# Even quarters for a one-hot table, two block products interleaved, and two more multiplications of zeros in a two-layer graph attention kernel

## The chip, the core and the metric

The kernel runs on one core of one Trainium2 chip. Times are microseconds of device time for one execution. The names of the engines in the profile are PE (TensorE, matrix products), PEld (its weight loads), DVE (VectorE), ACT (ScalarE), POOL (GpSimd) and SP (SyncE, which issues most transfers).

## The reference

A graph of 512 nodes has 16,896 edges (`src`, `dst`), sorted by `dst`, one self loop for each node among them. Two graph attention layers run over it; the second has one head, and the result is added to `x` and normalised.

```python
def gat_layer(x, W, a_s, a_d, b, edge_index, concat):
    h = (x @ W).reshape(n, H, C)
    alpha_s = jnp.einsum('nhc,hc->nh', h, a_s)
    alpha_d = jnp.einsum('nhc,hc->nh', h, a_d)
    e = leaky_relu(alpha_s[src] + alpha_d[dst], 0.2)
    e = jnp.exp(e - segment_max(e, dst)[dst])
    alpha = e / (segment_sum(e, dst)[dst] + 1e-16)
    return segment_sum(h[src] * alpha[:, :, None], dst) + b
...
h = elu(gat_layer(x, W1, ...))       # x 512x768, W1 768x6144, 8 heads of 768
out = gat_layer(h, W2, ...)          # W2 6144x768, 1 head
return layernorm(x + out)
```

## The kernel before

The kernel never walks the edges one by one. It first counts, for each pair of destination and source, how many edges there are (`cnt`, 512x512), and then treats attention as dense matrices, head by head: projection of `x`, logits, a softmax weighted with the counts, the aggregation, and the second layer's product of this head, all summed up. Large products are done by a scheme with seven block products instead of eight, P1 to P7, each on blocks of 256 rows by 384 by 384; a block product has two halves of 128 rows (`i` = 0 and 1) and three chunks of 128 along the sum (`HK` = 3). A product in float32 of one chunk shows in the trace as two passes of TensorE, so one half of a block product is six passes.

Instructions are not reordered: each engine runs its own in the order in which the Python code issues them, and waits for others by semaphores where data require it. The changed stage is the first 62 us, in which three things are interleaved by hand on all engines:

- **Loading and turning x.** x arrives in pieces, in the order written out at the start of the kernel: left halves of row blocks 0 and 1, the left half of the first weights (three chunks), right halves of the row blocks, and so on. `turn_x(t, r)` transposes a half row block by three products with the identity (line 213) into a bank of the pool `mm`, and ScalarE copies it into `xT` (line 214). Before that, `keep_warm(n)` issues n multiplications of zeros of 128x128 by 128x512 (line 184) that nobody reads.
- **The first projection** (`first_projection`, head 0). Its list `items` holds fourteen steps, P1, P2, P5, P3, P6, P7 and P4, each for `i` = 0 and 1; a step multiplies (line 309, through `product`) and empties its bank, on ScalarE by a copy (line 430) or on VectorE by an addition (line 432). P1 has banks of the pool `held`, since P6, P7 and P4 add to them later. `turns` says after which step more of x is turned: two groups after the first step, four after the third.
- **Counting.** Edges lie in 132 chunks of 128 (`EC`). For each chunk there is a one-hot of its sources (`os`, 128x512, made on VectorE at line 528 or on ScalarE at line 526, from a pool of 32 buffers) and one or two one-hots of its destinations within blocks of 32 nodes, in the table `od`. TensorE multiplies the two (line 554) and sums over chunks. VectorE makes `od` in four quarters (`destinations`, line 507) by comparing `rel`, the destination less the block's first node, with `offsets`. A quarter has 33 chunks; the columns written are rounded outwards to even ones, so each quarter's write has 34 columns, one of which belongs to a neighbour:

```python
def destinations(lo, hi):
    lo, hi = lo // 2 * 2, (hi + 1) // 2 * 2
```

The loop over nine `batches` issues, in turn: the quarter of `od` that is new, the VectorE one-hots of the batch, some additions for later products (`extra`, among them `inside`, lines 513 and 514, which checks the destinations, and the sums of x, lines 289 to 292), the steps of the projection up to `wants[n]` with ScalarE's one-hots between them, and the counting (`count`). On ScalarE the step `nidx` (line 611), which its one-hots need, stands after the first step of the projection.

Of the kernel before, what the change touches and what calls it, by code (L numbers as in the profile page):

```python
# [8 lines left out]
F32 = mybir.dt.float32  # L9
F16 = mybir.dt.float16  # L10
BF16 = mybir.dt.bfloat16
# [3 lines left out]
ALU = mybir.AluOpType  # L15
# [21 lines left out]
def gat_pass(  # L37
# [16 lines left out]
    nc = tc.nc  # L54
    P = 128
    N, D = x.shape
    H = a_src1.shape[0]
    E = src.shape[0]
    NT = N // P
    DC = D // P  # L60
    HALF = D // 2
    EC = E // P
    EH = EC // 2
    HK = DC // 2
# [14 lines left out]
    ohp = counting.enter_context(tc.tile_pool(name="onehot", bufs=1))  # L79
# [3 lines left out]
    held = counting.enter_context(tc.tile_pool(name="held", bufs=2, space=bass.MemoryType.PSUM))  # L83
# [88 lines left out]
    B0, additions0 = sums_by_dma(W1[0], w1_0, "w1")  # L172
# [9 lines left out]
    def keep_warm(n):  # L182
        for _ in range(n):
            nc.tensor.matmul(idle, zeros[:, :P], zeros, start=True, stop=True)

    keep_warm(5)
    nodes = ohp.tile([P, N], F16, name="nodes")
    nc.gpsimd.iota(nodes, pattern=[[1, N]], base=0, channel_multiplier=0,
                   allow_small_or_imprecise_dtypes=True)
# [8 lines left out]
    for j in range(2):  # L198
        nc.vector.tensor_reduce(picks[:, j:j + 1], ident.rearrange("p (j k) -> p k j", k=32)[:, j, :], axis=AX.X,
                                op=ALU.add)  # L200
# [8 lines left out]
    def turn_x(t, r):  # L209

        ps = mm.tile([P, 512], F32, name="mm")
        for k in range(HK):
            nc.tensor.transpose(ps[:, k * P:(k + 1) * P], x_sb[:, t, (r * HK + k) * P:(r * HK + k + 1) * P], ident)  # L213
        nc.scalar.copy(xT[:, r * HK:(r + 1) * HK, t * P:(t + 1) * P],
                       ps[:, :HALF].rearrange("p (k n) -> p k n", n=P))


    general = flag is None
    idx_f = ohp.tile([EH, 2, 2, P], F32, name="idx_f")
    if general:  # L220
        nc.vector.tensor_copy(idx_f, idx_i)
        idx = ohp.tile([P, 2, EC], F32, name="idx")
        psi = tr.tile([P, 512], F32, name="tr")
        for j in range(2):
            for r in range(2):
                nc.tensor.transpose(psi[:, (2 * j + r) * EH:(2 * j + r + 1) * EH], idx_f[:, j, r, :],
                                    ident[:EH, :EH])
        nc.vector.tensor_copy(idx, psi[:, :2 * EC].rearrange("p (j c) -> p j c", j=2))
    else:

        B = 32
        blocks = []
        for c in range(EC):
            m = (c + 0.5) * P * N / E
            b = int(m // B)
            slack = 2 + 16 * (m / N * (1 - m / N)) ** 0.5
            lo, hi = b - (m - b * B < slack), b + ((b + 1) * B - m < slack)
            blocks.append(range(max(lo, 0), min(hi, N // B - 1) + 1))  # L240
        assert max(map(len, blocks)) <= 2


        base = ohp.tile([P, 2, EC], F32, name="base")
        for k in range(2):
            firsts = [b[k] if k < len(b) else None for b in blocks]
            lo = 0
            while lo < EC:
                hi = lo + 1
                while hi < EC and firsts[hi] == firsts[lo]:  # L250
                    hi += 1
                nc.gpsimd.memset(base[:, k, lo:hi], float(2 * N if firsts[lo] is None else firsts[lo] * B))
                lo = hi
        offsets = ohp.tile([P, B, 2, EC // NT + 1], F16, name="offsets")
        nc.vector.tensor_copy(offsets.rearrange("p b k c -> p b (k c)"),
                              nodes[:, :B].unsqueeze(2).to_broadcast([P, B, 2 * (EC // NT + 1)]))
        nc.vector.tensor_copy(idx_f, idx_i)
        turn_x(0, 0)
        turn_x(1, 0)
        psi = tr.tile([P, 512], F32, name="tr")  # L260
        for j in range(2):
            for r in range(2):
                nc.tensor.transpose(psi[:, j * EC + r * EH:j * EC + (r + 1) * EH], idx_f[:, j, r, :], ident[:EH, :EH])
        rel = ohp.tile([P, 2, EC], F16, name="rel")
        nc.vector.tensor_tensor(rel, psi[:, :EC].unsqueeze(1).to_broadcast([P, 2, EC]), base, op=ALU.subtract)
        idx = ohp.tile([P, EC], F32, name="idx")
        nc.vector.tensor_copy(idx, psi[:, EC:2 * EC])

# [140 lines left out]
        nc.vector.tensor_tensor(cnt[:, t, :], steps[:, 1:], steps[:, :N], op=ALU.subtract)  # L409
        nc.scalar.activation(absent[:, t, :], cnt[:, t, :], AF.Relu, bias=far, scale=NO_EDGE)  # L410

    def first_projection(h, XA, B_):


        HS[h] = hs = hpool.tile([P, NT, D], F32, name="hs")
        new_alpha(h)
        bank = {}

        def step(p, over, i, out, op):
            def multiply():  # L420
                if over is None:
                    bank[p, i] = (held if p == "P1" else mm).tile([P, 512], F32, name="held" if p == "P1" else "mm")
                else:
                    bank[p, i] = bank[over, i]
                product(bank[p, i], XA, B_, p, i, over is None)

            def empty():
                ps, o = bank[p, i][:, :HALF], out(i)
                if op is None:
                    nc.scalar.copy(o, ps)  # L430
                else:
                    nc.vector.tensor_tensor(o, o, ps, op=op)
            return multiply, empty, op is not None

        steps = [
            ("P1", None, lambda i: hs[:, i, L], None),
            ("P2", None, lambda i: hs[:, i, L], ALU.add),
            ("P5", None, lambda i: hs[:, 2 + i, R], None),
            ("P3", "P5", lambda i: hs[:, i, R], None),
            ("P6", "P1", lambda i: hs[:, i, R], ALU.subtract),  # L440
            ("P7", "P1", lambda i: hs[:, 2 + i, R], ALU.subtract),
            ("P4", "P1", lambda i: hs[:, 2 + i, L], None),
        ]
        return [step(p, over, i, out, op) for p, over, out, op in steps for i in range(2)]

    def spread(h):
        BC[h] = tr.tile([P, 512], F32, name="tr")
# [36 lines left out]
        nc.scalar.activation(nb1T, psb[:, :H * DC], AF.Copy, scale=-1.0)  # L484

    XA, xsums = left(xT, xS)
    items = first_projection(0, XA, B0)
    again = None
    if not general:

# [9 lines left out]
            hits[b] = hits.get(b, 0) + 1  # L500
        todo = dict(hits)
        cps, done = {}, set()
        od = ohp.tile([P, B, 2, EC], BF16, name="odw", bufs=1)

        def destinations(lo, hi):
            lo, hi = lo // 2 * 2, (hi + 1) // 2 * 2
            nc.vector.tensor_tensor(od[:, :, :, lo:hi], rel[:, :, lo:hi].unsqueeze(1).to_broadcast([P, B, 2, hi - lo]),
                                    offsets[:, :, :, :hi - lo], op=ALU.is_equal)

        def inside():  # L510

            below = ohp.tile([P, 2, EC], F16, name="below")
            nc.vector.tensor_scalar(below, rel, float(B), None, op0=ALU.is_lt)
            nc.vector.scalar_tensor_tensor(below, rel, 0.0, below, op0=ALU.is_ge, op1=ALU.mult, accum_out=found)

# [2 lines left out]
        def by_steps(b):  # L518
            return b * B // P == S
# [23 lines left out]
        def count(batch, rest):  # L543


            for c, b in ((c, b) for c in batch for b in blocks[c]):
                queues[b * B % P // B].append((c, b, hot[c, by_steps(b)]))
            while any(queues) and (rest or all(queues) or sum(map(len, queues)) > 3):
                for c, b, h_ in [q_.pop(0) for q_ in queues if q_]:
                    t, r = b * B // P, b * B % P  # L550
                    if t not in cps:
                        pool, name = (bc, "bc") if t == S else (tr, "tr")
                        cps[t] = pool.tile([P, 512], F32, name=name)
                    nc.tensor.matmul(cps[t][r:r + B, :N], od[:, :, b - blocks[c][0], c], h_,  # L554
                                     start=todo[b] == hits[b], stop=todo[b] == 1,
                                     tile_position=(0, r), skip_group_check=True)
                    todo[b] -= 1
            for t in range(NT):
                if t not in done and all(todo[b] == 0 for b in range(t * P // B, (t + 1) * P // B)):
                    (counted_by_steps if t == S else counted)(t, cps[t])  # L560
                    done.add(t)


        turns = {1: [(0, 1), (1, 1)], 3: [(2, 0), (3, 0), (2, 1), (3, 1)]}
        keep_warm(1)
        found = const.tile([P, 1], F32, name="found")
        wholes = len(items)
# [17 lines left out]
        pos, made, quarter, waiting = 0, set(), EC // NT, []  # L585
        for n, batch in enumerate(batches):
            for k in sorted({c // quarter for c in batch} - made):
                destinations(k * quarter, (k + 1) * quarter)
                made.add(k)
            sources(kinds(batch, False), waiting)  # L590
            ahead = kinds(batches[n + 1], True) if n + 1 < len(batches) else []
# [5 lines left out]
            while n < len(wants) and pos < wants[n]:  # L597
# [3 lines left out]
                multiply, empty, on_vector = items[pos]  # L601
# [17 lines left out]
            if n + 1 == len(batches):  # L619
                spread(0)  # L620
                q = [lift(0, t) for t in range(NT)]
# [11 lines left out]
    else:  # L633
# [26 lines left out]
        q = [lift(0, t) for t in range(NT)]  # L660
# [187 lines left out]
    for h in range(H - 1):  # L848
# [39 lines left out]
        q = [lift(h + 1, 0)]  # L888
# [36 lines left out]
        if h + 2 < H:  # L925
            B_, sums = right(W1[h + 2], "w2")
# [90 lines left out]
    q, rden = [lift(H, 0)], []  # L1017
# [34 lines left out]
    for t in range(NT):  # L1052
# [61 lines left out]
```

## Time and profile before

| | us |
|---|---|
| median of 3 runs | 647.89 |
| lowest, highest | 646.70, 647.94 |
| the profiled execution | 647.22 |
| its span, first to last instruction | 645.4 |
| TensorE busy | 634.1 |
| VectorE busy | 517.4 |
| ScalarE busy | 280.1 |
| GpSimd busy | 46.1 |

The profile is of one execution, so durations and starts belong to that one. A row of the timeline merges instructions of one kind that follow each other; its start is that of the first, its duration reaches to the end of the last, and a bracket at its end tells how long the engine had been idle and what ended that. A pass of TensorE is pipelined, so the next can begin before its modelled end.

### The profile page before, as it was taken

The page shows a single profiled execution, that of the slowest core. Times are in us where ns is not written, and L with a number is a line of the kernel's source. Part 1 is how long each engine was busy: PE and PEld are TensorE (multiplying, and loading weights), DVE is VectorE, ACT ScalarE, POOL GpSimd, SP SyncE. Part 2 cuts the span into 40 slices and gives each one's busy share as a digit, 9 for nine tenths or more (in the row PEclk, how much of TensorE's full clock was granted, in tenths as well). Part 3 has the DMA queues.
Part 4 walks back from the last instruction along what each step waited for, and adds up shares of the span by engine and source line. Part 5 has one row for each costly group of instructions (what it writes and reads, how often), then busy time and mean ns, then how long its engine had stood idle before and what let it go on. Part 6 is the DMA issues. An engine that isn't in the chain of part 4 may idle for free.

```text
span 645.4 us, 7150 instructions
## 1 busy us (share of the span) xinstructions
PE 634.1 (98%) x2327; PEld 402.4 (62%) x2327; DVE 517.4 (80%) x1128; ACT 280.1 (43%) x472; POOL 46.1 (7%) x89
## 2 busy tenths in 40 slices
PE   8999999999999999999999999999999999999995
PEld 5555585556855586556855586556855586544553
DVE  8799989978689678878689678878689678876775
ACT  5865744530726035530726035530725035543440
POOL 1300011010000110011000110010000110000000
PEclk9999999999999999999999999999999999999999
DMA  8993488696715794196715794196815990410222
GB/s 297 326 230 87 74 248 270 151 256 193 188 55 135 187 257 139 27 259 187 188 56 134 188 258 138 29 258 193 185 54 139 233 258 16 107 50 0 30 60 77
DMA packets 81096, 100.32 MB, mean 155 GB/s; under 512 B 39654, under 2 KB 63006, under 8 KB 81054
## 3 DMA queue, kind: packets, MB, share of 16 engines
q1 hardware_dynamic: 67646, 78.57, 39.8%
q0 software_dynamic: 12976, 20.65, 18.4%
q10 hardware_dynamic: 432, 0.59, 0.3%
q8 instruction: 20, 0.33, 0.2%
q14 instruction: 22, 0.18, 0.1%
HBM read 86.93 MB, written 1.59 MB: 137 GB/s over the span
## 4 chain that ended last, share of the span: by engine, by line
PE 94%; DVE 4%; ACT 1%; DMA 1%; issue 0%; DVEq 0%; ACTq 0%
PE mm L309 62%; PE mm L779 20%; PE mm L725 3%; PE mm L1060 3%; PE held L309 2%; PE tr L554 1%; DVE os L528 1%; DMA hs<-in_x_dram 1%; PE mm L213 0%; PE bc L554 0%; DVE scr L318 0%; PE tr L984 0%; DVE h L365 0%; DVE q L475 0%; DVE q L470 0%
## 5 line engine op out<-in xcount | busy, mean ns | idle before, releaser
L309 PE MATMUL mm<-w,gT 128*128 128x384 f32 x288 | 96.8, 488 | 0.2 <-DVE u L365 0.2
L309 PE MATMUL mm<-w,xT 128*128 128x384 f32 x264 | 88.2, 487 | 0.0
L309 PEld LDWEIGHTS mm<-w,gT 128*128 128x128 f32 x288 | 54.3, 190 | 38.1 <-issue 1.6
L309 PEld LDWEIGHTS mm<-w,xT 128*128 128x128 f32 x264 | 49.9, 190 | 35.3 <-ACT os L526 0.8
L783 ACT COPY u<-mm 128x256 f32<-128x256 f32 x21 | 7.8, 372 | 140.5 <-PE mm L779 140.5
L477 ACT ACTIVATE q<-q,nmax 128x512 f32<-128x512 f32 x36 | 25.8, 721 | 95.4 <-DVE nmax L475 95.4
L779 PE MATMUL mm<-PT,hs 128*128 128x256 f32 x252 | 61.3, 379 | 0.0
L309 PE MATMUL mm<-w1t,gS 128*128 128x384 f32 x180 | 60.6, 486 | 0.0
L309 PE MATMUL mm<-w2t,xS 128*128 128x384 f32 x168 | 56.6, 487 | 0.0
L779 PEld LDWEIGHTS mm<-PT,hs 128*128 128x128 f32 x252 | 47.8, 190 | 8.4 <-issue 0.4
L309 PEld LDWEIGHTS mm<-w1t,gS 128*128 128x128 f32 x180 | 34.1, 190 | 24.2 <-issue 0.6
L367 DVE TENSOR_TENSOR h<-h,mm 128x384 f32<-128x384 f32 x72 | 39.1, 550 | 12.5 <-PE mm L309 12.0
L309 PEld LDWEIGHTS mm<-w2t,xS 128*128 128x128 f32 x168 | 31.8, 190 | 22.4 <-ACT q L466 0.4
L779 PE MATMUL mm<-pS,gS 128*128 128x256 f32 x168 | 43.2, 380 | 0.0
L707 ACT COPY PT<-zr 128x1024 uint16<-128x1024 uint16 x34 | 39.5, 1161 | 2.6 <-DMA zr<-pS 2.0
L779 PEld LDWEIGHTS mm<-pS,gS 128*128 128x128 f32 x168 | 31.8, 190 | 4.7 <-DVE pS L752 0.4
L702 ACT COPY pS<-q 128x1024 uint16<-128x1024 uint16 x26 | 27.2, 1045 | 16.6 <-DVE q L687 16.6
L309 PE MATMUL mm<-w1t,gT 128*128 128x384 f32 x96 | 32.4, 487 | 0.5 <-DVE h L365 0.5
L309 PE MATMUL mm<-w,gS 128*128 128x384 f32 x96 | 32.6, 486 | 0.0
L309 PE MATMUL mm<-w,xS 128*128 128x384 f32 x96 | 32.5, 487 | 0.0
L367 DVE TENSOR_TENSOR u<-u,mm 128x384 f32<-128x384 f32 x28 | 15.4, 553 | 18.8 <-PE mm L309 18.7
L108 POOL DMA_DIRECT2D w1t<-in_L_gnn_W_dram x7 | 8.9, 1267 | 302.3 <-DVE hs L742 173.5
(187 smaller groups left out, 1080.5 us busy)
## 6 DMA issues: line engine op xcount, KB each, us to landing
w<-in_L_gnn_W_dram SPq DMA_DIRECT2D x91, 384.0 KB
w<-in_L_gnn_W_dram POOLq DMA_DIRECT2D x16, 576.0 KB, 8.7
w2t<-in_L_gnn_W_dram SPq DMA_DIRECT2D x10, 576.0 KB
w1t<-in_L_gnn_W_dram SPq DMA_DIRECT2D x9, 576.0 KB
w2t<-in_L_gnn_W_dram POOLq DMA_DIRECT2D x8, 576.0 KB, 8.8
w1t<-in_L_gnn_W_dram POOLq DMA_DIRECT2D x7, 576.0 KB, 8.3
a_s<-in_L_gnn_a_src_dram SPq DMA_DIRECT2D x8, 384.0 KB
a_d<-in_L_gnn_a_dst_dram SPq DMA_DIRECT2D x8, 384.0 KB
```

What stands on the lines that cost most here:

```text
L108: nc.gpsimd.dma_start(t1, upper[:, :, R], accum_op=ALU.add)
L309: nc.tensor.matmul(ps[:, :HALF], A_[p][:, k, i * P:(i + 1) * P], B_[p][:, k, :], start=start and k == 0, stop=k == HK - 1, skip_group_chec ...
L367: nc.vector.tensor_tensor(a, a, ps, op=ALU.subtract if p == "P7" else ALU.add)
L477: nc.scalar.activation(q, q, AF.Exp, bias=nmax, scale=-1.0)
L528: nc.vector.tensor_scalar(o, nodes, idx[:, c:c + 1], None, op0=ALU.is_equal)
L554: nc.tensor.matmul(cps[t][r:r + B, :N], od[:, :, b - blocks[c][0], c], h_, start=todo[b] == hits[b], stop=todo[b] == 1, tile_position=(0, ...
L702: nc.scalar.copy(apart.rearrange("p (h n) -> p h n", h=2), q.bitcast(U16).rearrange("p (n h) -> p h n", h=2))
L707: nc.scalar.copy(PT.rearrange("p s n -> p (s n)").bitcast(U16).rearrange("p (s n h) -> p s n h", s=NT, h=2)[:, :, t * P:(t + 1) * P, :], p ...
L725: nc.tensor.matmul(ps[:, :N], HS[h][:, s, c * P:(c + 1) * P], PT[:, s, :], start=(s == 0), stop=(s == NT - 1))
L779: nc.tensor.matmul(bank[p][:, :HN], A_[p][:, k, c * P:(c + 1) * P], B_[p][:, k, :], start=over is None and k == 0, stop=k == 1, skip_group ...
L783: nc.scalar.copy(u, part("P1"))
L1060: nc.tensor.matmul(ps[:, :cols.stop - cols.start], PT[:, s, t * P:(t + 1) * P], h2[:, s, cols], start=(s == 2), stop=(s == 1))
```

## The change

Three edits, all in the first stage; the order of all other instructions on every engine is as before:

- The table `od`, and `rel` with it, get a dimension of quarters, each padded from 33 to 34 chunks. A quarter's write covers its own columns alone. The padding of `rel` is set to -1 by one more memset on GpSimd, so that it matches no offset. `below` covers the padding too.
- The two halves of P1 run chunk by chunk in turn (chunk 0 of both, chunk 1 of both, chunk 2 of both) instead of one after the other. The two groups of transposes that stood between the halves stand before chunk 2. Both halves are emptied after that; ScalarE's copies of xT now come before its first copy of P1.
- `keep_warm(7)` in place of `keep_warm(5)` at the start.

```diff
-    keep_warm(5)
+    keep_warm(7)
...
+        QC = EC // NT
+        QW = QC + QC % 2
         base = ohp.tile([P, 2, EC], F32, name="base")
+        rel = ohp.tile([P, 2, NT, QW], F16, name="rel")
...
+        if QW > QC:
+            nc.gpsimd.memset(rel[:, :, :, QC:], -1.0)
+        offsets = ohp.tile([P, B, 2, QW], F16, name="offsets")
...
-        rel = ohp.tile([P, 2, EC], F16, name="rel")
-        nc.vector.tensor_tensor(rel, psi[:, :EC].unsqueeze(1).to_broadcast([P, 2, EC]), base, op=ALU.subtract)
+        nc.vector.tensor_tensor(rel[:, :, :, :QC],
+                                psi[:, :EC].rearrange("p (q c) -> p q c", c=QC).unsqueeze(1).to_broadcast([P, 2, NT, QC]),
+                                base.rearrange("p k (q c) -> p k q c", c=QC), op=ALU.subtract)
...
+        def firsts():
+            for k in range(HK):
+                if k == HK - 1:
+                    between()
+                for i in range(2):
+                    if k == 0:
+                        bank["P1", i] = held.tile([P, 512], F32, name="held")
+                    nc.tensor.matmul(bank["P1", i][:, :HALF], XA["P1"][:, k, i * P:(i + 1) * P], B_["P1"][:, k, :],
+                                     start=k == 0, stop=k == HK - 1, skip_group_check=True)
+
+        items = [step(p, over, i, out, op) for p, over, out, op in steps for i in range(2)]
+        for i, multiply in enumerate((firsts, lambda: None)):
+            items[i] = (multiply, *items[i][1:])
+        return items
...
+    def rest_of_x():
+        if not general:
+            for t in range(2):
+                turn_x(t, 1)
+
+    items = first_projection(0, XA, B0, rest_of_x)
...
-        od = ohp.tile([P, B, 2, EC], BF16, name="odw", bufs=1)
-
-        def destinations(lo, hi):
-            lo, hi = lo // 2 * 2, (hi + 1) // 2 * 2
-            nc.vector.tensor_tensor(od[:, :, :, lo:hi], rel[:, :, lo:hi].unsqueeze(1).to_broadcast([P, B, 2, hi - lo]),
-                                    offsets[:, :, :, :hi - lo], op=ALU.is_equal)
+        od = ohp.tile([P, B, 2, NT, QW], BF16, name="odw", bufs=1)
+
+        def destinations(q_):
+            nc.vector.tensor_tensor(od[:, :, :, q_, :], rel[:, :, q_, :].unsqueeze(1).to_broadcast([P, B, 2, QW]),
+                                    offsets, op=ALU.is_equal)
...
-            below = ohp.tile([P, 2, EC], F16, name="below")
+            below = ohp.tile([P, 2, NT, QW], F16, name="below")
...
-                    nc.tensor.matmul(cps[t][r:r + B, :N], od[:, :, b - blocks[c][0], c], h_,
+                    nc.tensor.matmul(cps[t][r:r + B, :N], od[:, :, b - blocks[c][0], c // QC, c % QC], h_,
...
-        turns = {1: [(0, 1), (1, 1)], 3: [(2, 0), (3, 0), (2, 1), (3, 1)]}
+        turns = {3: [(2, 0), (3, 0), (2, 1), (3, 1)]}
...
-                destinations(k * quarter, (k + 1) * quarter)
+                destinations(k)
```

More of the change, by code (lines that the diff above doesn't have):

```diff
@@ L253, in gat_pass @@
                 lo = hi
-        offsets = ohp.tile([P, B, 2, EC // NT + 1], F16, name="offsets")
+        if QW > QC:
+            nc.gpsimd.memset(rel[:, :, :, QC:], -1.0)
+        offsets = ohp.tile([P, B, 2, QW], F16, name="offsets")
         nc.vector.tensor_copy(offsets.rearrange("p b k c -> p b (k c)"),
-                              nodes[:, :B].unsqueeze(2).to_broadcast([P, B, 2 * (EC // NT + 1)]))
+                              nodes[:, :B].unsqueeze(2).to_broadcast([P, B, 2 * QW]))
         nc.vector.tensor_copy(idx_f, idx_i)
@@ L410, in counted_by_steps, with first_projection @@
         nc.scalar.activation(absent[:, t, :], cnt[:, t, :], AF.Relu, bias=far, scale=NO_EDGE)
-    def first_projection(h, XA, B_):
+    def first_projection(h, XA, B_, between):
         HS[h] = hs = hpool.tile([P, NT, D], F32, name="hs")
@@ L443, in first_projection @@
         ]
-        return [step(p, over, i, out, op) for p, over, out, op in steps for i in range(2)]
+        def firsts():
[11 more added lines that the diff above has]
+        return items
     def spread(h):
@@ L486, in gat_pass @@
     XA, xsums = left(xT, xS)
-    items = first_projection(0, XA, B0)
+    def rest_of_x():
[3 more added lines that the diff above has]
+    items = first_projection(0, XA, B0, rest_of_x)
     again = None
```

## The prediction

> **What bounds the kernel now.** I read the page first (its busy row and the shares of the chain that ended last), then TensorE's waits in the first 90 us, then the timeline of that stretch engine by engine, because every line of the diff lies there.
>
> ```profile
> span 645.4 us, 7150 instructions
> PE 634.1 (98%) x2327; PEld 402.4 (62%) x2327; DVE 517.4 (80%) x1128; ACT 280.1 (43%) x472; POOL 46.1 (7%) x89
> PE 94%; DVE 4%; ACT 1%; DMA 1%; issue 0%; DVEq 0%; ACTq 0%
> ```
>
> ```profile
> 62.00:640.00 578.00, 575.94 (x1983) 370.12 (x1982) 462.89 (x974) 240.84 (x401) 35.52 (x28) 1.00 0.56 147
> ```
>
> The second fence is the busy time by engine between 62 and 640 us, TensorE first. TensorE works 575.94 of those 578.00 us, on work that the diff doesn't touch. A microsecond that TensorE gains or loses before 62 us therefore moves the end by a microsecond, and nothing else counts. The profiled execution took 647.22 us, 1.82 more than its span; I sum against 647.22 and leave those 1.82 alone. The median shown is 647.89, 0.67 above it; the three times run from 646.70 to 647.94 (1.24 us).
>
> TensorE's waits in the first 90 us, in total, times and longest:
>
> ```profile
> PE mm L213 <- DMA hs<-in_x_dram: 0.8, 1, 0.8
> PE held L309 <- DVE hs L432: 0.7, 2, 0.4
> ...
> PE mm L213 <- ACT xT L214: 0.2, 1, 0.2
> ...
> PE mm L628 <- ACT xT L214: 0.2, 1, 0.2
> ```
>
> These are small. The larger loss is not called a wait; it is in TensorE's timeline (start, duration, line, tiles, count, idle before):
>
> ```profile
> 1.28 2.31 PE L184 MATMUL bc<-zeros 128*128 128x512 bf16 x5 [1.28 <-DVE zeros L179]
> 4.38 1.51 PE L213 MATMUL mm<-ident,hs 128*128 128x128 f32 x6 [0.79 <-DMA hs<-in_x_dram]
> 6.55 2.96 PE L309 MATMUL held<-w,xT 128*128 128x384 f32 x6
> 9.36 0.82 PE L213 MATMUL mm<-ident,hs 128*128 128x128 f32 x6
> 10.01 2.10 PE L309 MATMUL held<-w,xT 128*128 128x384 f32 x6
> 11.95 2.10 PE L309 MATMUL mm<-w,xT 128*128 128x384 f32 x6
> 13.88 0.82 PE L213 MATMUL mm<-ident,hs 128*128 128x128 f32 x6
> 14.94 0.93 PE L213 MATMUL mm<-ident,hs 128*128 128x128 f32 x6 [0.24 <-ACT xT L214]
> 16.06 0.16 PE L628 MATMUL mm<-ones,found 128*1 128x1 f32 x1 [0.18 <-ACT xT L214]
> ```
>
> ```profile
> 7.20 0.34 PEld L309 LDWEIGHTS held<-w,xT 128*128 128x128 f32 x1 [0.30 <-issue]
> 7.83 0.34 PEld L309 LDWEIGHTS held<-w,xT 128*128 128x128 f32 x1 [0.30 <-issue]
> 8.39 0.51 PEld L309 LDWEIGHTS held<-w,xT 128*128 128x128 f32 x2 [0.21 <-issue]
> ```
>
> Six transposes take 1.51 us at 4.38 and 0.82 at 9.36. Six passes of a block product (a float32 product of three chunks runs as six) take 2.96 at 6.55 and 2.10 at 10.01. Weight loads follow each other by 0.63 us (7.20 to 7.83), while at full speed six passes take 11.95 - 10.01 = 1.94, or 0.323 each. So TensorE ran at half speed until some moment between 7.83 and 8.39; I call it 8.3. (The granted clock of the windows reads 1.00 there: it doesn't show this, the pitch does.) From 4.38 to 14.5 no row carries an idle time: TensorE is the bound throughout. The speed rose 3.45 to 4.01 us after the idle 0.79 us ended at 4.38.
>
> **Seven multiplications.** Each costs at most 2.31/5 = 0.46 us, so seven end by 4.51 at the latest; the first transposes began at 4.38 because their data came then. Cost: 0 to 0.13 us; I take 0, since the 2.31 contain the pipeline's tail once. What they change is the gap: work is unbroken from 1.28 instead of 4.38. If unbroken work raises the speed, that can come at 1.28 + 3.45 = 4.73 at the earliest. The moment also seems to move between executions: the times spread over 1.24 us, which at half speed is 2.48 us of the moment, and the profiled time lies 0.52 above the lowest, or 1.04 us of it. The same place after the change is 4.73 + 1.04 = 5.8.
>
> [...]
>
> **Row blocks in turn.** No instruction is added: the same twelve passes, ordered chunk by chunk, with the two transpose groups before the third chunk (after eight passes). On ScalarE the order changes, and this is the part that speaks against the change:
>
> ```profile
> 9.56 0.48 ACT L430 COPY hs<-held 128x384 f32<-128x384 f32 x1 [3.15 <-PE held L309]
> 9.93 0.87 ACT L214 COPY xT<-mm 128x384 f32<-128x384 f32 x2
> 10.67 0.34 ACT L611 ACTIVATE nidx<-idx 128x132 f32<-128x132 f32 x1
> 11.11 1.33 ACT L526 ACTIVATE os<-nodes,nidx 128x512 bf16<-128x512 f16 x2
> 12.35 0.46 ACT L430 COPY hs<-held 128x384 f32<-128x384 f32 x1
> 12.71 1.33 ACT L526 ACTIVATE os<-nodes,nidx 128x512 bf16<-128x512 f16 x2
> 14.41 0.86 ACT L214 COPY xT<-mm 128x384 f32<-128x384 f32 x2 [0.37 <-PE mm L213]
> ```
>
> Now ScalarE empties the first product at 9.56 and does the rest while TensorE computes. Afterwards that copy waits until nearly the end of both products, and behind it stand the nidx step, four one-hots and the second copy, and behind those the copy of xT for which TensorE waits at 14.94. From the rows: copy 0.37 (9.56 to 9.93), nidx 0.44 (10.67 to 11.11), two one-hots 1.24 (11.11 to 12.35), copy 0.36 (to 12.71), two one-hots 1.33; together 3.74 us.
>
> With the speed rising at 5.8: the work between 5.8 and 6.55 halves, so the products begin at 6.55 - 0.37 = 6.18. Eight passes at 0.323 give 8.76, six transposes (10.01 - 9.36 = 0.65) 9.41, two passes 10.05, their drain 0.16 (2.10 - 1.94) 10.21. ScalarE's 3.74 us end at 13.95, and TensorE resumes 0.53 later (14.94 - 14.41) at 14.48 instead of 14.94. **Gain 0.46 us.** TensorE itself would be there at 9.41 + 4 x 0.323 + 1.94 + 0.65 = 13.29: 1.2 us are lost to ScalarE. Each microsecond of the moment is worth 0.5 us: at 4.73 the gain is 1.0, and with the moment unchanged at 8.3 a loss of 0.79 stands there instead.
>
> Data for an earlier start: the busy time and rate from the start,
>
> ```profile
> 0.00:5.70 5.70, 3.63 (x12) 1.83 (x13) 3.43 (x9) 1.69 (x2) 2.88 (x54) 1.00 0.62 199
> 0.00:8.40 8.40, 6.33 (x20) 3.62 (x21) 5.39 (x13) 2.24 (x3) 2.88 (x54) 1.00 0.75 248
> ```
>
> 199 GB/s over 5.7 us are 1.13 MB. The indices (2 x 67 KB), the left halves of two x blocks and three chunks of the weights (5 x 197 KB) are 1.12 MB, so those chunks are there at 5.7, before 6.18. By 8.4, 2.08 MB: the next five pieces too, before 8.76 plus a product. Cost 0; if that cover went, at most the 0.5 us by which the start moves.
>
> **Padding to 34.**
>
> ```profile
> 1.85 1.75 POOL L252 MEMSET base<- 128x10 f32 x47
> 6.99 1.28 DVE L507 TENSOR_TENSOR odw<-rel,offsets 128x2176 bf16<-128x2176 f16 x1
> 12.39 0.22 DVE L513 TENSOR_SCALAR below<-rel 128x264 f16<-128x264 f16 x1
> 12.65 0.43 DVE L514 SCALAR_TENSOR_TENSOR below<-rel,below 128x264 f16<-128x264 f16 x1
> 18.64 0.94 DVE L289 TENSOR_TENSOR xS<-xT 128x768 f32<-128x768 f32 x1
> 23.78 0.61 DVE L528 TENSOR_SCALAR os<-nodes,idx 128x512 bf16<-128x512 f16 x2
> 28.69 1.29 DVE L507 TENSOR_TENSOR odw<-rel,offsets 128x2176 bf16<-128x2176 f16 x1 [4.30 <-PE tr L554]
> 36.13 1.01 DVE L432 TENSOR_TENSOR hs<-hs,held 128x384 f32<-128x384 f32 x2
> 36.73 4.14 PE L309 MATMUL held<-w,xT 128*128 128x384 f32 x12 [0.44 <-DVE hs L432]
> 42.14 4.14 PE L309 MATMUL held<-w1t,xT 128*128 128x384 f32 x12 [0.25 <-DVE hs L432]
> ```
>
> A quarter already writes 2176 elements (34 chunks), so it keeps its 1.28 us. One more memset on GpSimd costs 1.75/47 = 0.04 us; it ends by 3.7, and the first odw, which now waits for it, starts at 6.99. The two `below` steps grow from 264 to 272 elements, 3% of 0.65 us, 0.02 us, and TensorE asks for their result only at 16.06. All nothing on the path.
>
> What goes is a wait: the third odw write, at 28.69, begins on an even column that belongs to the quarter before it, and so waits 4.30 us until TensorE has counted with that column. Without overlap VectorE goes on at 24.39 (the end of the row at 23.78). The following one-hots now wait singly for their 32 buffers, last read by counts one or two batches back, which are done by then. VectorE's next deadline is the pair at 36.13, for which TensorE waited 0.44 us; with up to 4.3 us of lead it waits for TensorE instead. **Gain 0.44 us.** The 0.25 us at 42.14 I leave standing; if they went too, the sum would be 0.25 lower. Earlier on, VectorE's sums must follow: s1 ends at 19.58, and the product that needs it ran at 20.9, so a gain of up to 1.3 us passes.
>
> Sum: 647.22 - 0.46 - 0.44 = 646.3 us.
>
> **The rivals.**
> [...] Chance 0.20.
> The speed does not rise earlier at all (multiplications of zeros don't count, or the moment is fixed): 647.22 + 0.79 - 0.44 = 647.6. For it: five multiplications in 2.31 us raised nothing by 4.38; against: they lasted less than 3.45 us. Chance 0.12.
> Slower: ScalarE becomes the gate. Its 3.74 us start only when the first product is done, whatever VectorE gains; it decides where the moment stays above 6.7, where the gain turns into loss. At 8.3, with the wait at 36.73 kept because the one-hots wait for buffers, 648.0, above the median; with the moment 1.44 us later (the rest of the spread), 648.7; with ScalarE late by twice 0.79, 649.5. For it: the 1.2 us lost to ScalarE even in my forecast; against: it needs a late moment and a kept wait. Chance 0.10, half of it above 649.2.
> More: ScalarE is not late, since its one-hots find gaps, and the moment is 4.73: (8.3 - 4.73)/2 + 0.44 = 2.2, 645.0. Chance 0.08.
>
> **How the numbers follow.** The forecast, moment 4.73 to 6.4, spans 645.8 to 646.6 and has 0.50. A measurement of this kernel tells about 0.2%, or 1.3 us, from no change: faster means below 646.6 and slower above 649.2. Faster: 0.50 + 0.08 and 0.02 of the first rival, 0.60. Slower: half of the third, 0.05. Same: the rest, 0.35. The range reaches from 645.1, by the last rival, to 647.8, just over the second.
>
> **What would show it.** Right: weight loads of the first products 0.32 us apart from before 6.5; no idle before the transposes at 4.4; a wait on the xT copy of about 1.2 us before the third transpose group, growing with an earlier rise; the third odw write directly behind the one-hots near 24; no idle before the products that began at 36.73. Wrong: half speed up to 8 again, or the transposes starting after 4.5, or VectorE idle for TensorE near 25 to 28.

## The result, and the profile after

The changed kernel takes 645.93 us (median of 14 runs, 645.58 to 646.71) against 647.77 for the kernel before (14 runs beside them, 645.45 to 648.18). The medians lie 1.84 us apart. The estimated ratio of the two kernels is 0.9981, with a 95% interval of 0.9972 to 0.9990, which is 1.2 us (0.6 to 1.8). The forecast was 646.3 in a range of 645.1 to 647.8. The profiled execution took 646.05 us, 1.17 less than the one of before.

The page of the changed kernel:

```profile
span 644.3 us, 7163 instructions
PE 633.2 (98%) x2329; PEld 401.8 (62%) x2329; DVE 517.5 (80%) x1128; ACT 280.0 (43%) x472; POOL 46.1 (7%) x90
PE 95%; DVE 3%; ACT 1%; issue 0%; DVEq 0%; ACTq 0%
```

In the shares of the chain that ended last, DMA's 1% has gone: the chain no longer begins with the load of the first piece of x. TensorE's timeline of the changed kernel (start, duration, line, tiles, count, idle before; L309 of before is L315 here, or L458 for the products in turn):

```profile
1.28 3.17 PE L184 MATMUL bc<-zeros 128*128 128x512 bf16 x7 [1.28 <-DVE zeros L179]
4.25 1.31 PE L213 MATMUL mm<-ident,hs 128*128 128x128 f32 x6
...
5.87 2.74 PE L458 MATMUL held<-w,xT 128*128 128x384 f32 x8
8.45 0.82 PE L213 MATMUL mm<-ident,hs 128*128 128x128 f32 x6
9.10 1.46 PE L458 MATMUL held<-w,xT 128*128 128x384 f32 x4
10.39 2.10 PE L315 MATMUL mm<-w,xT 128*128 128x384 f32 x6
12.33 0.82 PE L213 MATMUL mm<-ident,hs 128*128 128x128 f32 x6
14.09 0.93 PE L213 MATMUL mm<-ident,hs 128*128 128x128 f32 x6 [0.94 <-ACT xT L214]
```

```profile
35.36 4.14 PE L315 MATMUL held<-w,xT 128*128 128x384 f32 x12
40.77 4.14 PE L315 MATMUL held<-w1t,xT 128*128 128x384 f32 x12 [0.25 <-DVE hs L438]
...
60.74 4.14 PE L315 MATMUL mm<-w2t,xS 128*128 128x384 f32 x12
```

The gap of 0.79 us before the first transposes is closed (no idle before 4.25). They take 1.31 us against 0.82 at 8.45, part of it at half speed; eight passes take 2.74, a pitch of (8.45 - 5.87)/8 = 0.32, full speed from the start. Products begin at 5.87 instead of 6.55. Then TensorE stands still for 0.94 us before 14.09. From there it gains again: the products after the counts begin at 35.36 with no wait (36.73 before, after 0.44), and the last row, the same product as in this row of before, is 1.36 us earlier:

```profile
62.10 4.14 PE L309 MATMUL mm<-w2t,xS 128*128 128x384 f32 x12
```

Behind it the two kernels do the same work: 583.3 us to the end of the span before, 583.5 after. So the whole difference is made in three places: 0.85 us up to the third transposes (14.94 to 14.09), 0.52 from there to the products (21.79 us between them before, 21.27 after), and the rest behind 62 us, which took 0.2 longer in this execution.

The 0.94 us is explained by ScalarE of the changed kernel:

```profile
9.95 0.48 ACT L436 COPY hs<-held 128x384 f32<-128x384 f32 x1
10.32 0.32 ACT L635 ACTIVATE nidx<-idx 128x132 f32<-128x132 f32 x1
10.74 1.33 ACT L550 ACTIVATE os<-nodes,nidx 128x512 bf16<-128x512 f16 x2
11.98 0.46 ACT L436 COPY hs<-held 128x384 f32<-128x384 f32 x1
12.34 1.33 ACT L550 ACTIVATE os<-nodes,nidx 128x512 bf16<-128x512 f16 x2
13.58 0.84 ACT L214 COPY xT<-mm 128x384 f32<-128x384 f32 x2
```

From 9.95 to the copy at 13.58 it never stops: 3.63 us of work that could begin only when the first product in turn was done. And VectorE of the changed kernel:

```profile
22.49 1.40 DVE L552 TENSOR_SCALAR os<-nodes,idx 128x512 bf16<-128x512 f16 x5
23.80 1.29 DVE L531 TENSOR_TENSOR odw<-rel,offsets 128x2176 bf16<-128x2176 f16 x1
25.00 3.24 DVE L552 TENSOR_SCALAR os<-nodes,idx 128x512 bf16<-128x512 f16 x12
...
33.87 0.56 DVE L438 TENSOR_TENSOR hs<-hs,held 128x384 f32<-128x384 f32 x1 [1.38 <-PE held L315]
```

The third odw write stands directly behind one-hots (it waited 4.30 us for TensorE before), and VectorE then waits for TensorE, not the other way round.

### The profile page after: what moved, and what is told of

Same layout as the page of the kernel before. It is cut to its first block, busy times and chain, and to the rows that moved or that the text cites. A ratio compares the mean times of both kernels' runs of the same rounds, so it can differ in the third digit from the quotient of the medians.

```text
span 644.3 us, 7163 instructions
## 1 busy us (share of the span) xinstructions
PE 633.2 (98%) x2329; PEld 401.8 (62%) x2329; DVE 517.5 (80%) x1128; ACT 280.0 (43%) x472; POOL 46.1 (7%) x90
## 4 chain that ended last, share of the span: by engine, by line
PE 95%; DVE 3%; ACT 1%; issue 0%; DVEq 0%; ACTq 0%
PE mm L315 62%; PE mm L803 20%; PE mm L749 3%; PE mm L1084 3%; PE held L315 2%; PE tr L578 1%; PE bc L184 1%; PE held L458 1%; PE bc L578 0%; DVE scr L324 0%; ACT os L550 0%; PE mm L213 0%; PE tr L1008 0%; DVE h L371 0%; DVE q L495 0%
## 5 line engine op out<-in xcount | busy, mean ns | idle before, releaser
L315 PE MATMUL mm<-w,gT 128*128 128x384 f32 x288 | 96.8, 488 | 0.2 <-DVE u L371 0.2
L315 PE MATMUL mm<-w,xT 128*128 128x384 f32 x264 | 88.2, 487 | 0.0
L315 PEld LDWEIGHTS mm<-w,gT 128*128 128x128 f32 x288 | 54.3, 190 | 38.1 <-issue 1.6
L315 PEld LDWEIGHTS mm<-w,xT 128*128 128x128 f32 x264 | 49.9, 190 | 35.3 <-ACT os L550 0.8
L315 PE MATMUL mm<-w1t,gS 128*128 128x384 f32 x180 | 60.6, 486 | 0.0
L315 PE MATMUL mm<-w2t,xS 128*128 128x384 f32 x168 | 56.6, 487 | 0.0
L315 PEld LDWEIGHTS mm<-w1t,gS 128*128 128x128 f32 x180 | 34.1, 190 | 24.2 <-issue 0.6
L315 PEld LDWEIGHTS mm<-w2t,xS 128*128 128x128 f32 x168 | 31.8, 190 | 22.4 <-ACT q L486 0.4
L315 PE MATMUL mm<-w1t,gT 128*128 128x384 f32 x96 | 32.4, 487 | 0.5 <-DVE h L371 0.5
L315 PE MATMUL mm<-w,gS 128*128 128x384 f32 x96 | 32.6, 486 | 0.0
L315 PE MATMUL mm<-w,xS 128*128 128x384 f32 x96 | 32.5, 487 | 0.0
```

What stands on the lines that cost most here:

```text
L315: nc.tensor.matmul(ps[:, :HALF], A_[p][:, k, i * P:(i + 1) * P], B_[p][:, k, :], start=start and k == 0, stop=k == HK - 1, skip_group_chec ...
```

## The experiments

Twelve runs, each beside runs of the kernel before. The change has three parts: seven multiplications (`keep_warm`), two products in turn, padding. The first four runs put each alone into the kernel before, and two together.

**e1: seven multiplications alone.**

```
-    keep_warm(5)
+    keep_warm(7)
```

> Only keep_warm(7) is taken over. Theory A (the two extra multiplications close the gap before the transposes, so TensorE's speed rises earlier, and that is most of the gain): weight loads 0.32 us apart from about 5 to 6.5 us on, first block product from about 5.9 instead of 6.55, the third transpose group about 1.3 us earlier than 14.94 without a longer wait on ScalarE, the wait before the products at 36.7 kept at about 0.4 us; time about 1.3 us below before, 646.4. Rival B (the moment of the rise is not in the kernel's hands and was early in the changed kernel's profile by luck): median within 0.3 us of before, and half speed up to 7 us or later in most profiles.

646.10 us against 647.18, ratio 0.9983 (0.9975 to 0.9992). TensorE's timeline of this kernel:

```profile
6.00 2.10 PE L309 MATMUL held<-w,xT 128*128 128x384 f32 x6
...
13.52 0.93 PE L213 MATMUL mm<-ident,hs 128*128 128x128 f32 x6 [0.24 <-ACT xT L214]
```

The six passes take 2.10, not 2.96. One edited number gives nearly the whole gain, and the third transposes are earlier than in the full change. One expectation missed: the wait before the products after the counts did not stay at 0.4 us but was gone (34.99, table below), though the stretch from the third transposes to them, 21.47 us, is still 0.2 longer than with padding.

**e2: the turns alone** (`keep_warm(5)`, tables as before).

```
+        def firsts():
+            for k in range(HK):
+                if k == HK - 1:
+                    between()
+                for i in range(2):
...
-        turns = {1: [(0, 1), (1, 1)], 3: [(2, 0), (3, 0), (2, 1), (3, 1)]}
+        turns = {3: [(2, 0), (3, 0), (2, 1), (3, 1)]}
```

> Only the two halves of the first block product in turn. Theory A: no earlier rise, and ScalarE's copies, step and four one-hots stand behind the end of both halves, so TensorE waits for ScalarE before the third transpose group: 0.7 to 1.0 us slower than before, 648.5. Rival B (the interleaving is what gains, since weights come chunk by chunk): 0.5 us or more faster.

647.72 us, ratio 1.0007 (0.9997 to 1.0018): no gain, and by time no loss that can be told; 0.7 to 1.0 us had been expected, and the medians differ by 0.5. TensorE's timeline has the wait:

```profile
15.33 0.93 PE L213 MATMUL mm<-ident,hs 128*128 128x128 f32 x6 [0.94 <-ACT xT L214]
```

**e3: the padding alone.**

```
-        od = ohp.tile([P, B, 2, EC], BF16, name="odw", bufs=1)
+        od = ohp.tile([P, B, 2, NT, QW], BF16, name="odw", bufs=1)
...
-                destinations(k * quarter, (k + 1) * quarter)
+                destinations(k)
```

> Only the padding. Theory A: the third odw write starts near 24.4 instead of 28.7, the idle 0.44 us before the products at 36.7 goes, nothing else: 0.44 us faster, 647.3. Rival B (the one-hots now wait singly for their buffers, so that VectorE is no earlier where it counts): no difference, the idle time before those products stays.

647.02 us, ratio 0.9997 (0.9984 to 1.0009). In its trace the wait is gone:

```profile
15.40 0.93 PE L213 MATMUL mm<-ident,hs 128*128 128x128 f32 x6 [0.24 <-ACT xT L214]
...
36.68 4.14 PE L315 MATMUL held<-w,xT 128*128 128x384 f32 x12
```

From the third transposes to those products it is 21.28 us instead of 21.79, the 0.5 that was forecast, but this execution reached the transposes 0.46 later than that of before (its speed rose at 9.4 us, table below). The gain is seen in the trace and lies inside the noise of the times.

**e4: seven and padded, products in the old order.**

> keep_warm(7) and the padding, the first block product in its old order. Theory A: the whole gain of the earlier rise (1.3) and of the padding (0.44) without ScalarE's wait: 1.75 us below before, 646.0, and some 0.5 us faster than the changed kernel at the same moment of the rise. Rival B (the turns are needed for the earlier start): slower than the changed kernel's 645.9 by 0.5 us or more.

645.31 us, ratio 0.9971 (0.9959 to 0.9983): below the full change. TensorE's timeline:

```profile
14.02 0.93 PE L213 MATMUL mm<-ident,hs 128*128 128x128 f32 x6 [0.24 <-ACT xT L214]
...
35.30 4.14 PE L315 MATMUL held<-w,xT 128*128 128x384 f32 x12
```

Although its speed rose 1.4 us later than in the profile of the full change, it reaches the products at the same time. So the turns don't pay here. The runs that follow ask why, and repeat both kernels.

**e5: the full change, with ScalarE's early work issued earlier.**

```
     def rest_of_x():
+            nc.scalar.activation(nidx, idx, AF.Copy, bias=0.5, scale=-1.0)
+            for c in ahead[:3]:
+                one_hot(c, True)
+            del ahead[:3]
...
-                if pos == 1:
-                    nc.scalar.activation(nidx, idx, AF.Copy, bias=0.5, scale=-1.0)
```

> The changed kernel with ScalarE's nidx step and three of its one-hots issued before the copies of xT that stand ahead of the third chunk, where ScalarE was idle for 2.9 us, instead of behind the first product's copy. Theory A (the 0.94 us wait of the third transpose group is ScalarE's order alone): the wait falls to 0.24 us, 0.7 us below the changed kernel, about the time of seven multiplications with padding and the old order of the products. Rival B (the turns delay TensorE in another way, by banks or weights): the wait stays above 0.6 us and the time within 0.2 us of the changed kernel.

645.33 us, ratio 0.9973 (0.9963 to 0.9984). ScalarE's timeline, then TensorE's:

```profile
10.17 1.33 ACT L554 ACTIVATE os<-nodes,nidx 128x512 bf16<-128x512 f16 x2
```

```profile
13.53 0.93 PE L213 MATMUL mm<-ident,hs 128*128 128x128 f32 x6 [0.53 <-ACT xT L214]
```

The wait fell from 0.94 to 0.53, not to the 0.24 expected: two one-hots were still issued behind each copy, because the share of one-hots per step is worked out from those that are left; only the nidx step had left the chain. By the ratios this kernel is 0.5 us below the full change that ran beside it (e6, 0.9981).

**e6 and e7: the full change and e4's kernel once more, on one chip.**

> The changed kernel as it is, on the same chip and in the same rounds as the others. Theory A: 0.94 us wait before the third transpose group, no wait before the products near 35 to 36; the moment of the rise another one than in its first profile, between 4.6 and 8.1; median about 645.9. Rival B (the rise comes at a fixed 5.2 us in this program): 5.2 us again and a spread of times under 0.5 us.

> Seven multiplications and padding with the old order of the first product, again, beside the changed kernel. Theory A: 0.5 to 0.7 us below the changed kernel, with half its runs below 645.4. Rival B (its earlier median came from lucky moments of the rise in six runs): within 0.2 us of the changed kernel.

e6 took 646.31 us (0.9981, 0.9972 to 0.9990), e7 645.92 (0.9979, 0.9969 to 0.9989). The lead of e4's kernel was 0.6 us between e4 and the result above; here it is 0.4 between the medians and 0.1 by the ratios. The 0.5 to 0.7 us expected did not come, and two of e7's eleven runs lie below 645.4 where half were expected. The intervals overlap, so by time alone a lead isn't shown; that the old order reaches the third transposes earlier is read from the traces (table below). In e6 the speed rose 1.2 us earlier than in the first profile of the same kernel, so the program does not fix the moment. It brought only 0.16 us at the third transposes, which again waited for ScalarE:

```profile
4.13 1.06 PE L213 MATMUL mm<-ident,hs 128*128 128x128 f32 x6
...
13.93 0.93 PE L213 MATMUL mm<-ident,hs 128*128 128x128 f32 x6 [0.90 <-ACT xT L214]
```

**e8: the full change without the padding.**

> The changed kernel without the padding. Theory A (the padding takes 0.4 to 0.5 us out between the third transpose group and the products near 36, whatever else is changed): 21.7 us between those two starts instead of 21.3, and 0.4 us slower than the changed kernel. Rival B (the seven multiplications move TensorE and VectorE against the transfers so that this wait goes anyway, as with seven alone, where it was 21.47): no more than 0.2 us slower.

646.76 us, ratio 0.9996 (0.9987 to 1.0005), while the full change beside it had 0.9981. VectorE's timeline of e8, then TensorE's and GpSimd's:

```profile
27.62 1.29 DVE L525 TENSOR_TENSOR odw<-rel,offsets 128x2176 bf16<-128x2176 f16 x1 [3.96 <-PE tr L572]
28.83 4.54 DVE L546 TENSOR_SCALAR os<-nodes,idx 128x512 bf16<-128x512 f16 x12
```

```profile
36.33 4.14 PE L309 MATMUL held<-w,xT 128*128 128x384 f32 x12 [1.12 <-DVE hs L432]
```

```profile
27.90 0.91 POOL L168 DMA_DIRECT2D w1t<-w1t  x1 [7.32 <-DMA w1t<-w1t]
28.50 1.62 POOL L108 DMA_DIRECT2D w2t<-in_L_gnn_W_dram  x1
29.64 1.78 POOL L119 DMA_DIRECT2D w<-in_L_gnn_W_dram  x1
```

From the third transposes to the products it is 22.46 us, not the 21.7 expected. Twelve one-hots take 4.54 us here and 3.24 in the full change, and TensorE waits 1.12 us for what VectorE does next. In the same microseconds GpSimd issues three transfers, the last until 31.42. Taken singly, the five one-hots that start before 31.0 take 0.47 to 0.85 us each, and the seven from 31.46 on 0.33 to 0.34, about as in the kernel with padding. The two transfers issued at 28.50 and 29.64 land only 13.6 and 17.1 us after their issue, so moving the data does not slow a one-hot here; the late one-hots fall into the time of the issues. With padding the one-hots are nearly over (25.00 to 28.2) when GpSimd begins (28.07). This gave a theory of its own, tested by e11.

**e9: the full change with five multiplications.**

> The changed kernel with five multiplications again (turns and padding stay). Theory A: the rise falls back to 7 us or later in most executions, the third transpose group waits 0.9 us for ScalarE, the wait near 36 is gone: the turns' loss of 0.7 and the padding's gain of 0.5 cancel, within 0.4 us of before. Rival B (turns and padding bring the gain, the two multiplications little): 1 us or more below before.

647.27 us, ratio 0.9996 (0.9984 to 1.0007): without the two multiplications nothing measurable is left of the change. TensorE's timeline:

```profile
4.17 1.63 PE L213 MATMUL mm<-ident,hs 128*128 128x128 f32 x6 [0.58 <-DMA hs<-in_x_dram]
...
16.18 0.93 PE L213 MATMUL mm<-ident,hs 128*128 128x128 f32 x6 [0.94 <-ACT xT L214]
```

Beside e3, where the speed rose at nearly the same moment (9.40 and 9.48) without turns, the third transposes are 0.78 us later: the turns' price in this place.

**e10: e5, and one one-hot behind each copy instead of two.**

```
-            share = len(ahead) // (items_here + 1) if n == 0 else -(-len(ahead) // items_here)
+            share = 1 if n == 0 else -(-len(ahead) // items_here)
```

> The early ScalarE steps with one one-hot behind each copy of the first product instead of two. Theory A: the chain behind the first copy is 0.37 + 0.62 + 0.37 + 0.62 = 1.98 us, less than the 2.6 us that TensorE needs to the third transpose group, so the wait, 0.94 and then 0.53, falls to 0.24; 0.3 us below the early-steps kernel, and equal to seven multiplications with padding alone. Rival B: the wait stays near 0.5 because banks set it.

645.46 us, ratio 0.9969 (0.9960 to 0.9979). ScalarE's timeline, then TensorE's:

```profile
10.71 0.72 ACT L554 ACTIVATE os<-nodes,nidx 128x512 bf16<-128x512 f16 x1
...
13.25 0.86 ACT L214 COPY xT<-mm 128x384 f32<-128x384 f32 x2 [0.82 <-PE mm L213]
```

```profile
13.78 0.93 PE L213 MATMUL mm<-ident,hs 128*128 128x128 f32 x6 [0.24 <-ACT xT L214]
```

Now ScalarE waits for TensorE and the wait on the xT copy is the 0.24 of before: the 0.7 us was the order of issue on ScalarE. The 0.3 us below e5 that were expected can't be told by time (645.46 and 645.33, ratios 0.9969 and 0.9973). This order makes the turns harmless, not useful: 0.9969 is the level of e4 (0.9971) and e12.

**e11: e8 with a quiet GpSimd.** It leaves out GpSimd's accumulating transfers for the weights of the second head, two of the three issues seen in e8 among them; that head's weight sums are missing from its result.

```
-        nc.gpsimd.dma_start(t1, upper[:, :, R], accum_op=ALU.add)
+        if h != 1 or not slot == "w2" or general:
+            nc.gpsimd.dma_start(t1, upper[:, :, R], accum_op=ALU.add)
```

> The changed kernel without the padding, and without the accumulating transfers that GpSimd issues for the second head's weights (four of them between 28 and 31 us and later; that head's weight sums are left out of the result). Theory A (VectorE's twelve one-hots behind the third odw take longer while GpSimd issues transfers: 3.24 us ahead of them, 3.87 and 4.54 beside them): about 3.4 us, and the 1.12 us wait before the products near 36 shrinks to 0.2 or less. Rival B (they are long because they wait for buffers that TensorE still reads): 4 us or more, and the wait stays.

646.32 us, ratio 0.9980 (0.9971 to 0.9989). VectorE's timeline, then TensorE's:

```profile
29.59 3.23 DVE L549 TENSOR_SCALAR os<-nodes,idx 128x512 bf16<-128x512 f16 x12
```

```profile
35.90 4.14 PE L311 MATMUL held<-w,xT 128*128 128x384 f32 x12
```

The same one-hots without padding take 3.23 us, and the wait of 1.12 is gone, though the odw write still waited 3.96 us for TensorE (at 28.38). The stretch from the third transposes to the products is 21.27 us, as with padding. So without padding that wait alone costs nothing; it costs because it pushes the one-hots beside GpSimd's issues of transfers.

**e12: six multiplications and padding, products in the old order.**

> Six multiplications with the padding and the old order of the products: about 0.4 us of idle time stay before the transposes. Theory A (a stretch of 3.4 us needs to be busy for some four fifths, as the rises at 4.0 us after 80% and none after 75% say): as with seven, 645.3 to 646.0. Rival B (it must be unbroken): as with five and padding, about 647.0.

645.39 us, ratio 0.9967 (0.9956 to 0.9978). TensorE's timeline:

```profile
1.28 2.74 PE L184 MATMUL bc<-zeros 128*128 128x512 bf16 x6 [1.28 <-DVE zeros L179]
4.09 1.55 PE L213 MATMUL mm<-ident,hs 128*128 128x128 f32 x6
...
13.52 0.93 PE L213 MATMUL mm<-ident,hs 128*128 128x128 f32 x6 [0.24 <-ACT xT L214]
```

Six already close the gap, so the 0.4 us of idle time on which the expectation counted did not appear, and the run can't tell its two theories apart. This version and e4's, both simpler than the full change, have the ratios 0.9967, 0.9971 and 0.9979, the full change twice 0.9981; the intervals overlap, and which is the best of them the times don't settle.

**All profiles side by side.** The moment at which the speed rises is the time of the first entry in the trace's record of the granted clock (us from the span's start). Until that entry the windows read 1.00, although the pitch of the weight loads says half speed (in the kernel before 0.63 us, from 7.20 to 7.83, against 0.32 for a pass later); there the entry at 8.29 lies between 7.83 and 8.39, where the pitch changed. Then: start of the third transposes and their wait for ScalarE, start of the products after the counts and their wait for VectorE.

| kernel | multiplications | speed rises | third transposes, wait | products, wait |
|---|---|---|---|---|
| before | 5 | 8.29 | 14.94, 0.24 | 36.73, 0.44 |
| e2 turns | 5 | 7.89 | 15.33, 0.94 | 37.03, 0.37 |
| e3 padded | 5 | 9.40 | 15.40, 0.24 | 36.68, 0 |
| e9 turns, padded | 5 | 9.48 | 16.18, 0.94 | 37.45, 0 |
| e12 padded | 6 | 5.63 | 13.52, 0.24 | 34.79, 0 |
| e1 | 7 | 4.61 | 13.52, 0.24 | 34.99, 0 |
| e4 padded | 7 | 6.61 | 14.02, 0.24 | 35.30, 0 |
| e7 padded | 7 | 7.04 | 14.24, 0.24 | 35.51, 0 |
| e8 turns | 7 | 4.69 | 13.87, 0.94 | 36.33, 1.12 |
| e11 turns, quiet GpSimd | 7 | 6.08 | 14.63, 0.94 | 35.90, 0 |
| after (all) | 7 | 5.23 | 14.09, 0.94 | 35.36, 0 |
| e6 (all) | 7 | 4.02 | 13.93, 0.90 | 35.21, 0 |
| e5 (all, ScalarE earlier) | 7 | 4.81 | 13.53, 0.53 | 34.80, 0 |
| e10 (all, ScalarE spread) | 7 | 6.12 | 13.78, 0.24 | 35.06, 0 |

## Why the prediction was right, step by step

**The bound.** Right. What TensorE gained before 62 us (1.36 us) is what the profiled times differ by (1.17), within the 0.4 us by which the unchanged rest (583.15 to 583.55 us) varies over the fourteen profiles.

**Seven multiplications.** The mechanism was right and is shown: with five the speed rose at 7.9 to 9.5 in four profiles, with six or seven at 4.0 to 7.0 in ten, and e9, which takes them out of the full change, loses its gain. The moment was put at 5.8 and was 5.2 in the profile. That it came so near is in part luck: the ten profiles spread over 3 us, and where in this spread an execution falls the kernel does not set (5.23 and 4.02 in the two profiles of the full change). The first rival, with its chance of 0.20, stood for a rise after 6.4; with seven multiplications two of nine profiles have one, e4 (6.61) and e7 (7.04). Its latest moment, the 8.1 that e6's expectation names too, is shown by no run; the latest measured is e7's 7.04. Two bounds were off. "4.73 at the earliest" assumed that the 3.45 us begin with the first multiplication; e6 rose at 4.02. And "each microsecond of the moment is worth 0.5 us" does not hold for the earliest moments: e12 (5.63) and e1 (4.61) start the third transposes at the same 13.52. In e1 the next step, the transposes of the indices, waits 0.22 us for VectorE's idx_f. For later ones it holds: e4 to e7, 0.43 us of the moment are 0.22 at the third transposes.

**Row blocks in turn.** Chain, place and price were right: 3.74 us were forecast for ScalarE, 3.63 came. With the measured moment the forecast's own rule gives 14.48 - 0.5 x 0.6 = 14.18; it was 14.09. The 0.46 us of gain was the sum of two things that the prediction did not set side by side: 1.25 us for the earlier moment (8.3 to 5.8 at half a microsecond each) and a loss of 0.79 for the turns, which it names ("with the moment unchanged at 8.3"). The loss is what e9 and e3 show, 0.78. So its own numbers said that the multiplications alone would gain more than both together. Its 1.2 us "lost to ScalarE" are counted against TensorE without any wait, from start to start; there it measured 1.11 (12.33 + 0.65 to 14.09), of which 0.94 is the wait. One sign failed: the wait was to grow with an earlier rise, and it was 0.90 to 0.94 us in all six profiles in which ScalarE has the order of the change, for rises from 4.02 to 9.48. In the old order ScalarE does its copies while TensorE computes, and e1, e4, e7 and e12 keep the 0.24 wait. The rival "ScalarE becomes the gate" was thus true as a mechanism in these six profiles and decided nothing, because the multiplications gave more.

**Padding.** The gain of 0.44 came as 0.52 between the third transposes and the products, and the 0.25 at 40.77 stayed, as forecast. The step behind it was incomplete: it priced the wait of 4.30 us by the 0.44 that TensorE waited in one profile, as if it were fixed. e8 has a wait of 1.12 in the same place, and e11 shows what it hangs on: the one-hots behind the odw write run beside GpSimd's issues, which start when a sum for w1t has landed (27.9 to 28.8 in before, e1, e8 and e11). The 0.44 of before has the same cause, by the five traces without padding: the twelve one-hots take 3.23 us in e11, 3.55 in e1, 3.78 in e2, 3.87 in before and 4.54 in e8, and from the third transposes to the products it is 21.27, 21.47, 21.70, 21.79 and 22.46. In the last four the difference of the two is 17.92 us each time, so what the one-hots lose beyond about 3.35 us the products lose too. Without padding, part of the earlier start is given back here; with it, the stretch is 21.27 to 21.28 us in all nine profiles.

**The sum.** 646.3 forecast, 645.93 measured, 646.05 in the profiled execution. The terms were 0.46 and 0.44, a gain of 0.90; measured 0.85 and 0.52, less 0.2 in the unchanged rest, 1.17. Of the 0.39 by which the first term was too small, about 0.3 are the moment (5.23 for 5.8) and 0.1 ScalarE's chain (3.63 for 3.74). The measured median is nearer to the forecast than the gains are, 1.84 against 0.90 us, since the forecast was summed against a profile of 647.22 and the median of before was 647.77. The chances leaned on three times of before that spread over 1.24 us. In all its runs here they spread over 3.3 (645.1 to 648.5). No profile caught one of its low runs. The lowest lie where the lowest of e1 lies (645.12 and 645.24), so an early moment would fit them, and the piece of x does come at different times (gap of 0.79, 0.52, 0.49 and 0.58 us in the four profiles with five multiplications), but that is only argued and stays open.

## What to carry to other kernels

Where TensorE starts behind a load, count how long the filler work must last to join the first real work, and check the pitch of weight loads for the speed (0.63 us at half speed and 0.32 at full speed here): the sixth multiplication (e3 to e12, each beside its own runs of before) was worth 1.6 us in the medians, while the rebuilt order of two products gained nothing. An order that lets one engine work longer without a break can hold back the work of the next one that used to run beside it (TensorE's wait for ScalarE went from 0.24 to 0.94 us); list what is queued there in program order before moving it. A wait's price in one profile is not fixed: it depends on what runs beside the work that it delays (with the odw write 3.96 us late, the products waited 1.12 us in e8 and not at all in e11).

## What the runs showed of the hardware

**The speed changed on a grid of 3.41 us.** The windows view shows the clock falling back after the last work, in the kernel before and in the changed one (the 0.67 and 0.60 are the mean over half a microsecond):

```profile
643.00:643.50 0.50, 0.00 (x0) 0.00 (x0) 0.00 (x0) 0.00 (x0) 0.00 (x0) 0.67 0.03 9
```

```profile
640.00:640.50 0.50, 0.00 (x0) 0.00 (x0) 0.00 (x0) 0.00 (x0) 0.00 (x0) 0.60 0.36 133
```

By the trace's clock record it fell at 643.172 and 640.105, and rose at 8.293 and 5.226: 634.879 us apart in both. In all fourteen profiles the distance is 185, 186 or 187 times 3.4133 us (634.879/186), whatever the kernel. So in these profiles the changes of speed fit the ends of stretches of 3.41 us that do not start with the kernel, and the moment of the rise fits the end of the first stretch with enough work in it. With six or seven multiplications the stretch that ended in the rise began at 1.20 to 3.62 us in nine profiles and at 0.61 in e6; with five it began at 4.48 to 6.06, and the stretch ahead of it held the gap. How much work a stretch needs stays open, and the share of time with work does not decide it alone: in e6 one that began 0.67 us before the first multiplication (work in about 80% of it) sufficed, while in e9 one with a gap of 0.58 us in it (83%) and in e3 one with a gap of 0.49 us (86%) did not. The work in e6's was multiplications of zeros alone, in the other two mostly transposes; no run separates this from the place of the gap. Transposes counted in e11: the stretch from 2.66 to 6.08 was full, more than half of it with transposes, and the speed rose at its end.

**VectorE's one-hots took longer while GpSimd issued transfers.** The twelve one-hots take 3.23 to 3.24 us alone and 4.54 in e8 beside three issues, with the late ones all begun ahead of the end of the last issue. Not every one-hot beside an issue is late: of six in the changed kernel, between 29.03 and 31.26, three took 0.44 to 0.62 us and three 0.33 to 0.35. e8 and e11 agree that it is VectorE that is late beside these issues; by what mechanism, no run here shows.
